# Token sums earlier in one lasting tile, portions ahead of PV, and a projection spread over five periods

## The chip, the cores and the metric

The kernel runs on one core of a Trainium2 chip. The core has a matrix engine (TensorE, PE in the profile, with PEld for its weight loads), VectorE (DVE), ScalarE (ACT), GpSimd (POOL) and SyncE (SP), each with its own queue[...]. DMAs are issued from the queues of SP and POOL. The metric is the device time of one execution in microseconds, the median of several runs.

## What is computed

Two cross-attention layers follow each other for 8 batch elements. Queries are 100 tokens of 640 channels in 20 heads of 32. The context has 722 tokens of 1024 channels: 77 are text, 645 are image tokens ("ip"). Keys and values of both kinds are projected with weights of their own, and there are two softmaxes per head, over text and over image tokens. Layer 1 adds a term to the image logits and multiplies the image probabilities with a mask. Cut to what matters:

```python
# layer 0, for H = 20 heads
q = split(x @ Wq.T);  k, v = split(text @ Wk.T), split(text @ Wv.T)
k_ip, v_ip = split(ip @ Wk_ip.T), split(ip @ Wv_ip.T)
x = (attend(q, k, v) + attend(q, k_ip, v_ip)) @ Wo.T + bo + x
# layer 1, the same with its own weights, and
q_sem = softmax(q_all @ k_text_all.T * scale) @ text
sem = (q_sem @ ip.T) * scale
ip_probs = softmax(q @ k_ip.T * scale + 0.5 * sem) * mask
out = (softmax(q @ k.T * scale) @ v + ip_probs @ v_ip) @ Wout + bout + x
```

All data are fp32.

## The kernel before

A unit u is one batch element in one layer: units 0 to 7 are layer 0, 8 to 15 layer 1. Units go in pairs (`PAIRS`, eight of them). There are two kinds of work, interleaved by hand on TensorE, VectorE and ScalarE.

**Production** makes keys and values of image tokens, for a pair at a time, and writes them to scratch in DRAM (`k_d`, `v_d`, by POOL's DMAs). Image tokens are cut into five blocks of 128 (the last 133). Each block's product is a 2x2 block product in Winograd's form with seven products instead of eight (`seven`, in the order first, sixth, second, seventh, fifth, fourth, third). The rows of the 2x2 are the two units of the pair, so the seven products need sums of the two units' tokens: S1 and S2 (`token_sums`, lines 232 and 233, on VectorE), S4 (`fourth_sum`), and S3, which overwrites a quarter of x (`third_sum`). S1 feeds the fifth product, S2 the sixth, S4 the third. Values are made per block (`v_steps`, line 605, tiles psv_a to psv_e), keys for blocks (0, 1), (2, 3) and (4) together (`k_steps`, line 633, tiles psk). Each product is followed by an eviction from PSUM (lines 193 to 224). The sums of a group of blocks stand in a tile `s` from a pool with one buffer, made anew for each group; x stands in three places of one tile, refilled by SP's DMAs (line 166). The last pair is made differently, in visits: `two_chunks` (line 775, tiles psvk, sums sl) ten times, and `fifth_chunk` (line 814, psv) five times.

**Attention** goes in 80 periods, one for four heads of a unit (`ORDER`). In a period n TensorE does: the scores' first part against 512 tokens (line 976), transposes 0 to 3 of the probabilities of the period before (line 1067), the scores' second part, transposes 4 and 5, then PV of the period before (`values`, line 1089). VectorE takes the maxima (line 991 in layer 1) and copies transposes (line 1074; 2 and 4 go to ScalarE, line 1072), ScalarE makes the exponentials (line 999, 1018). What turns exponentials into probabilities stands in a list `later`: "portions" that call `factors` (lines 1021 to 1025), `scaled_rest` (1035, 1039) on VectorE and `scaled` (1031) on ScalarE. A portion is emitted before each production task that takes time, and what is left is emitted at the next period's first scores.

Small work is put between, too: for each pair of units the output projection in five pieces (`out_piece`, line 887, tile pso) and in layer 0 the next query projection. For the second last pair, the five pieces stood in period 71. The last pair's projection (`last_out`, line 939) is in period 79 and at the end. A planner (`spread`) gives each production task a due time so that all periods of a stretch have about the same TensorE work, small work counted; `between` emits tasks up to a time. Periods 70 to 79 belong to the last pair; production for it ends about period 73 (two_chunks) and 79 (fifth_chunk).

Of the kernel before, what the change touches and what calls it, by code (L numbers as in the profile page):

```python
# [15 lines left out]
B = 8  # L16
# [28 lines left out]
def two_layer_xattn(  # L45
# [113 lines left out]

    def load_x(us, j):  # L160

        n0, n1 = BLOCKS[j]
        at = placed[0] % NPLACE
        placed[0] += 1
        for i, u in enumerate(us):
            nc.sync.dma_start(
                x_all[:, at, i, :, : n1 - n0], ip_t[u % B].rearrange("k p n -> p k n")[:, :, n0:n1]
            )
        return at

# [323 lines left out]
    def load_res(g):  # L494

        us = PAIRS[g]
        l, b = divmod(us[0], B)
        t = one.tile([P, 2, NC_, S], F32, tag="res", name=f"res_{g}")
        n = len(us)
        if l == 0:  # L500
            nc.sync.dma_start(t[:, :n], x_t[:, b : b + n])
        else:
            nc.sync.dma_start(t[:, :n], x1_d[b // 2][:, b % 2 : b % 2 + n])
        resg[g] = t
# [29 lines left out]

    places, pair_marks = {}, {}

    def pair_tasks(us):

        l = us[0] // B
        g = PAIRS.index(us)  # L540
        tasks, at = [], places.setdefault(us, {})
        marks = pair_marks[us] = {}

        def load(j, us=us):
            places.setdefault(us, {})[j] = load_x(us, j)

# [6 lines left out]
        for js in ((0, 1), (2, 3), (4,)):  # L553
            n = BLOCKS[js[0]][1] - BLOCKS[js[0]][0]
            st, pos = {}, {}

            def begin(j, js=js, n=n, st=st, pos=pos):
                if j == js[0]:
                    st[0] = spool.tile([P, 3, HK, 2, NX], F32, tag="s", name=f"s_{us[0]}_{j}")
                pos[j] = int(len(js) == 2 and (j == js[0]) == (at[js[0]] > at[js[1]]))  # L560
                sums = [st[0][:, i, :, pos[j], :n] for i in range(3)]
                a11, a12, a21, a22 = quarters(at[j], n)
                token_sums(a11, a12, a21, a22, sums[0], sums[1], None, sums[2])

            def fourth_sum(j, n=n, st=st, pos=pos):
                s2, s4 = (st[0][:, i, :, pos[j], :n] for i in (1, 2))
                nc.vector.tensor_tensor(s4, quarters(at[j], n)[1], s2, ALU.subtract)

            def operands(which, j, js=js, n=n, st=st, pos=pos):

                if which in (3, 5, 6):
                    t = st[0][:, {5: 0, 6: 1, 3: 2}[which]]
                    if j is not None:
                        return lambda k: t[:, k, pos[j], :n]
                    return lambda k: t[:, k, :, :n]
# [128 lines left out]
            if first:  # L704
# [6 lines left out]
                tasks += v[:2] + [(0.0, text_sum)] + v[2:] + v_steps(1)  # L711
            else:
                for j in js:
                    tasks += head(j) + with_sums(j, v_steps(j))
                    marks[f"v {j}"] = len(tasks)
                    if j == NB - 1 and us[0] + 2 < B:
                        tasks.append((0.0, lambda: load_text([u + 2 for u in us])))
                tasks += ([] if l else k4_steps()) + ks_
            marks[f"k {js[-1]}"] = len(tasks)

            then = {0: ((us, 3), (us, 4)), 2: ((PAIRS[g + 1], 0), (PAIRS[g + 1], 1)), 4: ((PAIRS[g + 1], 2),)}
# [17 lines left out]
    def last_visits(visits):  # L739

        xs, lists = {}, []
        for i, (j, tasks_of) in enumerate(visits):

            def begin(i=i):
                if i == 0:
                    xs.update(places[LAST])
                elif i + 2 < len(visits):
                    xs[i + 2] = load_x(LAST, visits[i + 2][0])

            first_sums, tasks = tasks_of(j, xs, i)  # L750
            if first_sums and i:

                t, f = lists[-1][-1]
                lists[-1][-1] = (t, lambda f=f, g=first_sums: (f(), g()))
            lists.append([(0.0, begin)] + ([(0.0, first_sums)] if first_sums and not i else []) + tasks)
        return lists

    def two_chunks(r, j, xs, at):
        n0, n1 = BLOCKS[j]
# [3 lines left out]
        def begin():  # L763
            t = spool.tile([P, 3, HK, 2, NX], F32, tag="s", name=f"sl_{r}_{j}")
            a11, a12, a21, a22 = quarters(xs[at], n)
            s1, s2, s4 = (t[:, i, :, 0, :n] for i in range(3))
            sums.update(token_sums(a11, a12, a21, a22, s1, s2, None, s4))
            sums[7] = a21
            late.append(lambda: nc.vector.tensor_tensor(a21, a11, a21, ALU.subtract))
            late.append(lambda: nc.vector.tensor_tensor(s4, a12, s2, ALU.subtract))  # L770
            o[0] = opool.tile([P, 2, 2, P + NX], F32, tag="made", name=f"vko_{r}_{j}")

# [12 lines left out]
        def step(i):  # L785
            if i == 0:
                made[0] = seven(
                    f"psvk_{r}_{j}", product, tuple(o[0][:, h, m, : P + n] for h in range(2) for m in range(2))
                )
# [15 lines left out]

    def fifth_chunk(j, xs, at):
        open_ = {}

        def half(h):
# [3 lines left out]
            for k in range(NCC):  # L813
                nc.tensor.matmul(
                    ps[:, h * P : (h + 1) * P], lhsT=x_all[:, xs[at], h, k, :P],
                    rhs=wide[("wv00", "wv10")[k // HK]][:, k % HK, 2 * P : 3 * P],
# [5 lines left out]
            nc.scalar.copy(t, ps[:, : 2 * P].rearrange("p (i n) -> p i n", i=2))  # L822
            for i, u in enumerate(LAST):
                nc.gpsimd.dma_start(v_d[u][j * P : (j + 1) * P, 4 * P :], t[:, i])

# [48 lines left out]

    def load_wo(kind, src, g):
        for c in range(NC_):
            t = wpool.tile([P, NC_, P], F32, tag="wo", name=f"{kind}_{g}_{c}", bufs=3)
# [85 lines left out]
    def scores(u, c, part):  # L963
        k0, k1 = ((0, KA), (KA, NK))[part]
        if part == 0:
            emit(len(later))
            pr[u, c] = ppool.tile([S, 4, NK], F32, tag="p", name=f"p_{u}_{c}")
# [108 lines left out]
    def values(u, c):  # L1076
        g, at = group_of[u]
        if g not in hsg:
            hsg[g] = one.tile([P, 2, NC_, S], F32, tag="hs", name=f"hs_{g}")
        pt = pts[u, c]  # L1080
# [17 lines left out]
    def production():  # L1098
# [15 lines left out]
        def insert(i, *what):  # L1114
# [7 lines left out]
        v, k = asked("v", HC), asked("k", 2 * P)  # L1122
        insert(
            B // 2 - 1,
            ("v 4", 0, [(0.0, lambda: load_wv(wvi[1]))]),
            ("k 4", 1, v[:1]),
            ("k 4", 0, v[1:2] + [(0.0, lambda: load_quarters("k", wki[1], 2 * P))]),
        )
        insert(
            B // 2,  # L1130
            ("v 0", 7, v[2:3]), ("v 0", 6, v[3:]),
            ("v 1", 7, k[:1]), ("v 1", 6, k[1:2]), ("v 1", 5, k[2:3]), ("v 1", 3, k[3:]),
        )

        v_last = asked("v", 2 * P)
        insert(len(PAIRS) - 2, ("v 4", 0, [(0.0, last_weights)]), ("k 4", 2, v_last[:1]), ("k 4", 1, v_last[1:2]))
        for i, tasks in enumerate(all_tasks):
            plan.append((10 * i - AHEAD, 10 * i + 10 - AHEAD, tasks))
        n = 5 * LAST[0]
        every = list(range(NB))  # L1140
        visits = [(j, lambda j, xs, i, r=r: two_chunks(r, j, xs, i)) for r in range(2) for j in every]
        visits += [(j, fifth_chunk) for j in every]
        lists = last_visits(visits)

        lists[0][5:5] = v_last[2:3]
        lists[0][7:7] = v_last[3:]
        for a, b, tasks in (
# [35 lines left out]
    def small_work(n):  # L1183
# [21 lines left out]
        if n == len(ORDER) - 1:  # L1205
            for i in range(2):
                for ks_ in ((0, 1), (2, 3)):
                    at[2 * i + ks_[0] // 2].append((2.3, lambda i=i, ks_=ks_: last_out(i, ks_)))

        if u % 2 == 0 and 0 < u <= LAST[0]:  # L1210
            g = u // 2 - 1
            if p == 1:
                for i, c in enumerate(range(NC_)):
# [6 lines left out]
    def loads(n):  # L1220
        u, p = divmod(n, NC_)
        if u % 2 == 0 and 0 < u <= LAST[0]:
            g = u // 2 - 1
            if p == 0:
                load_wo("o", wo[PAIRS[g][0] // B], g)
            if p == 1 and g < B // 2:
                load_wo("q", wq[1], g)
        if n == NC_ * LAST[0] + 2:
            load_res(len(PAIRS) - 1)
# [16 lines left out]
    with tc.manual_schedule(engines={mybir.EngineType.PE, mybir.EngineType.DVE, mybir.EngineType.Activation}):  # L1246
        for _, f in pair_tasks(PAIRS[0]):
            f()
        load_q(0)
        load_vt(0)  # L1250
        load_k(0, 0)
        todo = production()
        done = [0]
# [35 lines left out]
        for n, (u, c) in enumerate(ORDER):  # L1289
# [15 lines left out]
            if n == NC_ * LAST[0] - 1:  # L1305
                load_q(LAST[1])
            between(n, 0.6, 0.8, at[2])
            if n < len(ORDER) - 2:
# [3 lines left out]
            if last:  # L1312
                transposes(*last, 4)
                transposes(*last, 5)
            between(n, 0.8, 1.0, at[3])
            if last:
                values(*last)
# [54 lines left out]
```

## Time and profile before

| | us |
|---|---|
| median of 3 runs | 2088.62 |
| lowest, highest | 2087.55, 2089.88 |
| profiled execution, whole | 2089.18 |
| its span, first to last instruction | 2087.4 |
| TensorE busy in it | 2041.9 (98%) |
| VectorE busy | 1119.4 (54%) |
| ScalarE busy | 785.1 (38%) |
| mean granted TensorE clock | 0.994 |

The busy time of matmuls is modelled[...]; so the share is no measure of how much work there is. The granted clock is that which the throttle allowed. "A <- B" in a list of waits means that an instruction of A stood still until one of B was done. In the chain of waits each step is the one that released the next. Second-layer production begins about 1108 us, production for the last pair about 1750 us, and the first scores of periods 71, 74 and 79 stand at 1948.42, 1995.10 and 2056.54 us.

### The profile page before, as it was taken

How to read it: one execution, taken by the hardware profiler on the slowest of the kernel's cores; microseconds unless marked ns; L12 is line 12 of the kernel's file. 1: busy time of each engine (PE TensorE's matmuls, PEld its weight loads, DVE VectorE, ACT ScalarE, POOL GpSimd, SP SyncE). 2: the span in 40 equal slices, each digit the busy share in tenths (PEclk: the TensorE clock that was granted, in tenths of full speed). 3: DMA queues.
4: the chain of work that ended last, by engine and by line, in shares of the span. 5: the costliest groups of instructions: out<-in, count | busy, mean ns of one | idle time of the engine just before them, and what ended most of it. 6: DMA issues, size and time to landing. Idle time of an engine off the chain costs nothing.

```text
span 2087.4 us, 38776 instructions
## 1 busy us (share of the span) xinstructions
PE 2041.9 (98%) x15154; PEld 1578.1 (76%) x15154; DVE 1119.4 (54%) x3053; ACT 785.1 (38%) x2255; POOL 309.1 (15%) x445
## 2 busy tenths in 40 slices
PE   9999999999999999999999999999999999999988
PEld 8676767776777877777777877786777678888866
DVE  2211222355555555555557566656565657777775
ACT  1001000134433333334433444434444445565565
POOL 3212312121111111111110011000101011111110
PEclk9999999999999999999999999999999999999998
DMA  9545223332422624225263443344333455545451
GB/s 329 151 133 168 81 74 94 94 95 82 112 84 87 169 78 119 83 81 162 75 166 116 142 127 108 94 135 122 111 103 110 114 141 142 164 126 146 125 152 38
DMA packets 296341, 252.20 MB, mean 121 GB/s; under 512 B 46623, under 2 KB 265171, under 8 KB 296159
## 3 DMA queue, kind: packets, MB, share of 16 engines
q1 hardware_dynamic: 274382, 181.29, 32.1%
q0 software_dynamic: 21776, 68.44, 9.2%
q8 instruction: 119, 1.95, 0.4%
q14 instruction: 64, 0.52, 0.1%
HBM read 180.74 MB, written 68.93 MB: 120 GB/s over the span
## 4 chain that ended last, share of the span: by engine, by line
PE 92%; DVE 5%; ACT 1%; issue 1%; DMA 0%; SPq 0%; DVEq 0%; ACTq 0%
PE psv_d L605 8%; PE pspt L1067 8%; PE psv_a L605 7%; PE psk_a L633 6%; PE psk_d L633 6%; PE sc L976 6%; PE pv L1089 5%; PE psv_e L605 4%; PE psv_b L605 4%; PE psv_c L605 4%; PE psk_c L633 3%; PE psk_b L633 3%; PE psk_e L633 3%; PE pso L887 3%; PE psk_d L666 2%; PE psq L275 2%
## 5 line engine op out<-in xcount | busy, mean ns | idle before, releaser
L999 ACT ACTIVATE p<-sc,st 100x512 f32<-100x512 f32 (+1 forms) x320 | 165.5, 529 | 216.8 <-DVE st L985 134.6
L1031 ACT ACTIVATE p<-p,st 100x512 f32<-100x512 f32 x320 | 207.6, 713 | 66.0 <-DVE st L1025 65.8
L1067 PE MATMUL pspt<-ident,p 100*128 100x100 f32 (+1 forms) x1920 | 217.6, 254 | 13.9 <-ACT p L1031 5.5
L1067 PEld LDWEIGHTS pspt<-ident,p 100*128 100x128 f32 (+1 forms) x1920 | 191.4, 139 | 52.0 <-ACT p L1031 8.6
L1074 DVE COPY pt<-pspt 128x400 f32<-128x400 f32 (+1 forms) x319 | 174.9, 568 | 103.5 <-PE pspt L1067 96.1
L999 ACT ACTIVATE p<-p,st 100x512 f32<-100x512 f32 (+1 forms) x320 | 176.6, 554 | 87.2 <-DVE st L991 87.2
L1072 ACT COPY pt<-pspt 128x400 f32<-128x400 f32 x161 | 79.1, 491 | 284.4 <-PE pspt L1067 284.0
L605 PE MATMUL psv_a<-wv,x 128*128 128x397 f32 (+1 forms) x560 | 185.5, 473 | 0.0
L654 POOL DMA_DIRECT2D k_d<-ko x140 | 99.5, 715 | 509.9 <-DVE ko L219 455.4
L605 PE MATMUL psv_d<-wv,s 128*128 128x320 f32 (+1 forms) x560 | 174.3, 454 | 0.0
L605 PEld LDWEIGHTS psv_a<-wv,x 128*128 128x128 f32 x560 | 103.1, 190 | 67.6 <-issue 12.6
L991 DVE CUSTOM_DVE_ANT_0 p<-sc,sem 100x512 f32<-100x512 f32 (+1 forms) x320 | 138.7, 490 | 20.0 <-PE sc L976 18.9
L605 PEld LDWEIGHTS psv_d<-wv,s 128*128 128x128 f32 x560 | 104.2, 190 | 54.7 <-issue 4.3
L976 PE MATMUL sc<-k,q 32*100 32x210 f32 (+1 forms) x1280 | 140.0, 507 | 0.9 <-DMA k<-k_d 0.9
L985 DVE TENSOR_REDUCE st<-sc 100x2 f32<-100x1024 f32 (+1 forms) x160 | 125.2, 824 | 28.6 <-PE sc L976 28.6
L620 POOL DMA_DIRECT2D v_d<-vo x70 | 38.8, 554 | 661.9 <-DVE gst L595 328.9
L633 PE MATMUL psk_d<-s,wk 128*128 128x256 f32 (+1 forms) x672 | 136.5, 348 | 0.0
L633 PE MATMUL psk_a<-x,wk 128*128 128x256 f32 (+1 forms) x672 | 135.7, 347 | 0.6 <-ACT ko L193 0.6
L633 PEld LDWEIGHTS psk_a<-x,wk 128*128 128x128 f32 x672 | 109.0, 189 | 21.3 <-issue 5.0
L633 PEld LDWEIGHTS psk_d<-s,wk 128*128 128x128 f32 x672 | 108.2, 189 | 18.5 <-issue 5.1
L605 PE MATMUL psv_b<-wvt,s 128*128 128x320 f32 x280 | 83.0, 439 | 11.5 <-DVE s L233 11.4
L605 PE MATMUL psv_e<-wvt,x 128*128 128x397 f32 (+1 forms) x280 | 92.6, 473 | 0.0
(227 smaller groups left out, 3319.8 us busy)
## 6 DMA issues: line engine op xcount, KB each, us to landing
x<-ip_t SPq DMA_DIRECT2D x80, 512.0 KB
k<-k_d SPq DMA_DIRECT2D x80, 322.5 KB
v<-v_d SPq DMA_DIRECT2D x80, 320.0 KB
v_d<-vo POOLq DMA_DIRECT2D x70, 320.0 KB, 2.6
k_d<-ko POOLq DMA_DIRECT2D x112, 128.0 KB, 4.8
o<-wo SPq DMA_DIRECT2D x35, 320.0 KB
x<-ip_t SPq DMA_DIRECT2D x20, 532.0 KB
q<-wq SPq DMA_DIRECT2D x20, 320.0 KB
```

The costliest lines, as they stand in the source:

```text
L605: nc.tensor.matmul(ps[:, :m], lhsT=tokens(k)[:, :P], rhs=w[:, k, :], start=(k == 0 and not go_on), stop=(k == HK - 1), skip_group_check=True,)
L633: nc.tensor.matmul(ps[:, i * m : (i + 1) * m], lhsT=W["k", WHICH[which]][:, k, r * P : (r + 1) * P], rhs=tokens(k), start=(i == 0 and k == ...
L654: nc.gpsimd.dma_start(dst[:, :, r], ko[0][:, h, :, i, p0 : p0 + n])
L976: nc.tensor.matmul(scs[i // 2][:S, i % 2, : k1 - k0], lhsT=qs_[u][rows, c, :], rhs=ks[u, c][rows, k0:k1], start=True, stop=True)
L985: nc.vector.tensor_reduce(st[:, part, 2 * h : 2 * h + 2], scs[h][:S, :, :n], AX.X, ALU.max, negate=True)
L991: nc.vector.tensor_tensor_reduce(out=p[:, i, k0 : k0 + n], in0=scs[h][:S, i % 2, :n], in1=sems[u][:, k0 : k0 + n], scale=-1.0, scalar=3.0e ...
L999: nc.scalar.activation(dst, dst if l else scs[h][:S, i % 2, :n], AF.Exp, bias=st[:, part, i : i + 1], scale=-1.0 if l else 1.0, accum_out= ...
L1031: nc.scalar.activation(p[:, i, :KA], p[:, i, :KA], AF.Copy, scale=mul[:, 0, i : i + 1])
L1067: nc.tensor.transpose(ps[:rows, i * S : (i + 1) * S], pr[u, c][:, i, j * P : j * P + rows], ident[:S, :S])
L1072: nc.scalar.copy(dst, src)
L1074: nc.vector.tensor_copy(dst, src)
L1089: nc.tensor.matmul(ps[32 * i : 32 * i + 32, :S], lhsT=lhs, rhs=pt[:rows, j, i * S : (i + 1) * S], start=(j == 0), stop=(j == 5),)
```

## The change

Five edits, with 30 lines more in all.

- The sums' tile `s_all` is made once and lasts. `head(j)`, which makes S1 and S2 of a block, is put two products ahead: a group's first head before the last two products of the group before (for the first group of a pair, of the pair before), a second block's head before the last two products of the first block. The visits of the last pair do the same. Some sums of weights move by a product to make room.
- The list of portions is emptied just before `values`, and no longer at the next period's first scores.
- From period 74 on, transposes 4 and 5 come straight after the second scores, ahead of the production or small work that is due there.
- The five pieces of the second last pair's output projection go one each into periods 74 to 78, and its weights are loaded one each in periods 72 to 76. For this the last pair's PV results and residual get tiles that others no longer need (`qst` and `wk4`).
- `place_of` computes where a block of x lies instead of remembering it.

```diff
+    s_all = spool.tile([P, 3, HK, 2, NX], F32, tag="s", name="s")
...
-        t = one.tile([P, 2, NC_, S], F32, tag="res", name=f"res_{g}")
+        pool, tag = (one, "res") if g < len(PAIRS) - 1 else (wpool, "wk4")
+        t = pool.tile([P, 2, NC_, S], F32, tag=tag, name=f"res_{g}")
...
+    def place_of(us, i):
+        return (NB * PAIRS.index(us) + i) % NPLACE
...
-                if j == js[0]:
-                    st[0] = spool.tile([P, 3, HK, 2, NX], F32, tag="s", name=f"s_{us[0]}_{j}")
...
             else:
+                if js[0]:
+                    tasks[ahead:ahead] = head(js[0])
+                else:
+                    first_sums[us] = head(0)
                 for j in js:
-                    tasks += head(j) + with_sums(j, v_steps(j))
+                    v = with_sums(j, v_steps(j))
+                    if len(js) == 2 and j == js[0]:
+                        v[-2:-2] = head(js[1])
+                    tasks += v
...
             marks[f"k {js[-1]}"] = len(tasks)
+            ahead = len(tasks) - 2
...
-            if first_sums and i:
-                t, f = lists[-1][-1]
-                lists[-1][-1] = (t, lambda f=f, g=first_sums: (f(), g()))
+            elif sums:
+                lists[-1][-2:-2] = [(0.0, sums)]
...
-    def load_wo(kind, src, g):
-        for c in range(NC_):
+    def load_wo(kind, src, g, chunks=range(NC_)):
+        for c in chunks:
...
         if part == 0:
-            emit(len(later))
...
-            hsg[g] = one.tile([P, 2, NC_, S], F32, tag="hs", name=f"hs_{g}")
+            hsg[g] = one.tile([P, 2, NC_, S], F32, tag="hs" if g < len(PAIRS) - 1 else "qst", name=f"hs_{g}")
...
+        for i in range(1, len(PAIRS) - 1):
+            insert(i, *wants.get(i, []), ("k 4", 2, first_sums[PAIRS[i + 1]]))
...
+        if NC_ * LAST[0] + 4 <= n < NC_ * LAST[0] + 4 + NC_:
+            at[0].append((1.7, lambda: out_piece(len(PAIRS) - 2, n - NC_ * LAST[0] - 4)))
...
-            if p == 1:
+            if p == 1 and u < LAST[0]:
...
+        if NC_ * LAST[0] + 2 <= n < NC_ * LAST[0] + 2 + NC_:
+            load_wo("o", wo[1], len(PAIRS) - 2, [n - NC_ * LAST[0] - 2])
...
-            between(n, 0.6, 0.8, at[2])
+            few = n >= NC_ * LAST[0] + 4
+            if not few:
+                between(n, 0.6, 0.8, at[2])
...
                 transposes(*last, 4)
                 transposes(*last, 5)
+            if few:
+                between(n, 0.6, 0.8, at[2])
             between(n, 0.8, 1.0, at[3])
+            emit(len(later))
             if last:
                 values(*last)
```

## The prediction

> **What bounds the kernel now.** I read four views in this order: the page's busy shares, TensorE's waits, the stretches of the last periods, the chain of waits there. The page has TensorE busy 2041.9 us of a 2087.4 us span, and the chain is 92% TensorE. No matmul is added or removed by the change, so it can win only TensorE's idle time (45.5 us) and time lost to a reduced clock. The waits of TensorE say whose it is (total us, times, longest):
>
> ```profile
> PE psv_b L605 <- DVE s L233: 11.4, 8, 2.9
> PE pspt L1067 <- ACT p L1031: 5.5, 14, 1.3
> PE psq L275 <- DMA wq<-wq: 4.7, 1, 4.7
> PE pspt L1067 <- DVE pt L1074: 3.4, 5, 0.8
> ...
> PE psvk_b L775 <- DVE sl L233: 1.1, 1, 1.1
> ```
>
> The first and last rows are one thing: nine times the second product of a block stands still for the token sum S2 of VectorE, 12.5 us in all. The timeline shows the worst:
>
> ```profile
> 1108.06 2.34 PE L605 MATMUL psv_a<-wv,x 128*128 128x320 f32 x8
> 1113.27 2.39 PE L605 MATMUL psv_b<-wvt,s 128*128 128x320 f32 x8 [2.87 <-DVE s L233]
> ```
>
> The block before ended at 1107.2, its last eviction waited behind attention work until 1109.49, and S1 ran only at 1111.71.
>
> The transposes' rows lie in the last ten periods. The stretches there (length, busy PE, PEld, DVE, ACT, POOL with counts, then granted clock) show two losses, idle time and a clock below 1.00:
>
> ```profile
> 1982.80:1995.10 12.30, 10.76 (x141) 9.15 (x137) 9.04 (x35) 8.24 (x25) 3.99 (x6) 1.00 1.00 285
> 1995.10:2005.90 10.80, 9.38 (x120) 7.41 (x120) 8.44 (x31) 8.64 (x25) 0.92 (x2) 1.00 0.79 216
> 2005.90:2019.30 13.40, 11.36 (x125) 9.11 (x120) 9.21 (x34) 8.85 (x25) 1.21 (x3) 0.87 0.32 92
> 2019.30:2033.00 13.70, 10.92 (x108) 8.12 (x104) 9.24 (x34) 8.48 (x24) 0.00 (x0) 0.75 0.19 53
> ```
>
> The chain of waits through one such period (start, us, what) shows that TensorE isn't the bound there; VectorE is in every second step:
>
> ```profile
> 2004.12 0.58 DVE pt L1074
> 2004.75 1.28 PE pv L1089 x48
> 2006.06 0.26 DVE hs L1093
> 2006.32 0.38 DVE st L1021
> ...
> 2007.50 0.71 DVE p L1039
> 2008.22 0.39 DVE p L1035
> 2008.60 0.60 DVE p L991
> ...
> 2011.05 0.50 DVE pt L1074
> 2011.59 1.05 PE pspt L1067 x8
> 2012.63 0.54 PE sc L976 x8
> ```
>
> The portions (L1021 to L1035, 2.3 us) stand in VectorE's queue behind the copy of PV, though the text exponentials that they need ended at 2004.43 (ScalarE, 2003.98 + 0.45). So portions and the next maxima (4 x 0.61) run one after the other, after PV.
>
> [...] L1021 starts 1.8 us after its input is there, right behind hs. [...] here the sums' pool has one tile, and S1 (1111.71) comes after the last product of the old block (1107.2). [...] 0.75 granted in the emptiest period[...]. [...] S1 and S2 measure 0.68 and 0.69, and those are used.
>
> **The change part by part**, against the profiled run's 2087.4 us of span (2089.18 in all, 1.8 outside the span, 0.56 above the median of 2088.62).
>
> *Sums earlier, one lasting tile.* 43 of the 45 heads (35 + 10 on line 232; the first two stay) go two products ahead. The first S1 and S2 then need only product 5 and older ones, and their place on VectorE is right behind product 5's eviction, which waits for that product anyway: no new wait on TensorE's results. Two products are 4.4 us or more of TensorE work in a pair, 3.6 in the last visits, plus what attention lies between; the longest stall is 2.87. So all nine waits fit under it: -12.5; I keep 1 for leftovers, **-11.5**. What it puts in front: S1+S2 = 1.37 us ahead of the evictions of products 4 and 3, and in many blocks ahead of the portions. The cover is product 4 itself (2.2 us): product 5's eviction 0.45 and the sums 1.37 make 1.8. No row of TensorE waits on those evictions now. The data: x of the third or fourth block was asked for a whole block earlier, now five products (11 us) before use instead of seven; only the two first sums wait for x today (3.9 us, start). Nothing. Weight sums slip by one product: nothing, same cover.
>
> *Portions before PV.* In periods with production tasks they were out already; the order moves there in one place. In the last periods and the tail they leave the loop, while PV (1.28) and the next scores (1.05) run.
>
> *Projection over periods 74 to 78, transposes 4, 5 right behind the second scores.* Five pieces of 1.69 leave period 71 (1948.4 to 1970.3), with 1.9 us of stalls there (0.91 + 0.32 + 0.17 + 0.49). The planner levels: production slips by about one product, and one half of a fifth-chunk task (1.9) moves from 74 to 73. Until the scores of period 74: -8.45 - 1.9 - 0.66 (PV in 73) - 0.9 (the k wait) + 1.9 = **-10**. The k wait: in 73 the last product ended 1985.76, k landed 1995.1, 9.3 us. After, TensorE has 0.7+1.9+0.7+0.55+1.9+0.8+1.9+1.2 = 9.6 between, so about 0; without that cover up to +2.
>
> Then the loop, from the copy of transpose 5 (time 0): PV to 1.4, scores to 2.4; VectorE portions to 2.3, hs, maxima to 5.2; ScalarE's scaling 1.3 to 3.8. A period with the piece alone (74, 76): first transposes 4.1 to 4.8, fifth-chunk half to 6.7 over the two copies, second transposes to 7.4, then scores, 2.4 of maxima, copy: 3.5. Total 10.9. With half task and piece together in front (75, 77, 78): transposes at 6.0, their copies one after the other to 7.65, scores at 8.1: 11.6. From the scores of 74 to those of 79: 6.05 (74) + 11.5 + 10.9 + 11.5 + 11.5 + 4.9 = 56.3 against 61.4 (1995.10 to 2056.54): **-5**. The piece of 1.69 goes where VectorE gave 2.3 free; PV still waits about 2.4 for transpose 5's copy where no half task is left in front of it.
>
> *Tail.* Before, the scaling waited for hs until 2072.99, and the transposes trickled 2073.77 to 2075.6. Its input, the text exponentials, ended at 2070.2, and they had themselves waited for the copy of transpose 4 (2067.71), which stood behind a projection. After, both waits go, and the projection runs meanwhile. Scores of 79 to the transposes 15.8 instead of 17.2; 24 transposes 3.5 instead of 6.0 at full clock; the end 6.6 instead of 7.5: **-5**.
>
> *Clock.* The sums above are for full clock. Before, half clock cost about 7.8 in 2013 to 2058 (psv 3.6 and 3.4 for 2.05, transposes 1.6 for 0.85, scores, PV) and 2.6 in the tail. Bounds afterwards 0 and 12; stalls of 2.4 us remain in three periods, so I take about half: **+6**.
>
> *Queues.* The five out writes (100 KB) and weight loads (320 KB) move with the pieces; VectorE's addition (0.4) is in the loop above. The last pair's residual gets its own place and is loaded near 1393: SP then waits for x_d (issued 1393.15, 5.0 to landing), between issues at 1393.45 and 1398.26: nothing is late. The two bias additions (1.99) move with it to a POOL that is idle until 1413.7.
>
> Sum: -11.5 - 10 - 5 - 5 + 6 = -25.5. A second way, by idle time: from 1948.4 on 19.2 idle and 10.4 clock go, 15.7 idle and 6 clock stay (2.4 x 3 + 0.9 x 3 + ... and about 5 at the end), -7.9, with the sums -19.4. The two differ by what stuttering matmuls hide in busy time. I take -23.5 from the median: **2065 us**.
>
> **Rivals.** (A) The end keeps its length: VectorE (9.2 busy of some 11 in such a period) stays the bound, or the clock trips as often. For it: 10.9 to 11.6 is hardly under today's undisturbed 10.8 to 11.9. Against: five pieces then run inside. Left: the sums and a few us, -13: 2076. (B) The denser end keeps the full clock: -31, 2058. For: the trips follow periods with 2 to 2.8 us idle. Against: three stalls of 2.4. (C) Slower: the sums expose evictions. VectorE is 60 to 75% busy in the second layer; a chunk of maxima ahead of product 5's eviction pushes it, the sums and product 4's eviction together, and the next block's first product then waits up to 1.37. It decides from 23.5 / 1.37 = 17 exposed heads of 43; with 25 it is +11: 2100. Against: the same 1.37 stands today ahead of the second product's eviction. (D) The lasting tile tracks strided parts as one and the early sums wait for product 3 after all: then VectorE stalls in order and TensorE gains nothing there, -12: 2077. Against: the first sums read and write parts whose last readers are products 5 and 6.
>
> **Chances.** Forecast 0.56 (own range 2059 to 2071), A 0.17, B 0.14, C 0.05, D 0.05, no change worth measuring 0.03. Range **2057 to 2077**: it takes in A and B and leaves C out. A change of 0.2% (4 us) is about what can be told from none: faster 0.92, same 0.03, slower 0.05.
>
> **What will show it.** Right: rows of psv_b and psvk_b behind s gone from TensorE's waits; pspt behind p L1031 near nothing; the last five periods at 11 to 11.6 with a projection in each; span of the stretch before 1995 some 20 us shorter. Wrong: new rows of psv or psk behind vo or ko evictions (C), a wait for k in period 74 above 1 us, granted clock below 0.8 over the last 80 us (A).

## The result and the profile after

The changed kernel takes 2060.6 us (median of 4 runs, 2060.31 to 2061.25); the kernel before took 2089.25 beside it (4 runs, 2087.55 to 2090.11). The ratio is 0.9864, its 95% interval 0.9847 to 0.9881: 28.65 us less. The forecast said 2065.0.

The waits of TensorE after (total us, times, longest):

```profile
PE psq L279 <- DMA wq<-wq: 5.3, 1, 5.3
PE pspt L1080 <- DVE res L906: 3.8, 13, 1.1
PE psv_b L613 <- DVE wvt L135: 2.9, 1, 2.9
PE pv L1103 <- DVE pt L1087: 2.4, 3, 0.8
...
PE sc L989 <- DMA k<-k_d: 0.9, 1, 0.9
```

The rows of psv_b and psvk_b behind s are gone, and so is the row of the transposes behind ScalarE's scaling (5.5 us before, 14 times). No row of a product behind a vo or ko eviction is larger than 0.6 us. What is new is psv_b behind a sum of weights, 2.9 us in one piece. The row of the transposes behind res, the residual's addition, grew from 2.1 us to 3.8.

The page shows how much the span lost, and that TensorE's busy time lost 13.7 us (2041.9 before), although there are as many matmuls:

```profile
span 2058.5 us, 38749 instructions
PE 2028.2 (99%) x15154; PEld 1568.4 (76%) x15154; DVE 1118.0 (54%) x3053; ACT 785.0 (38%) x2255; POOL 310.2 (15%) x445
```

Busy time that falls without work falling speaks for matmuls at a higher clock, which the stretches show (before, the 40 matmuls pv<-pt,v of a period took 1.07 us at 1.00, from 2070.18, and 1.90 at 0.50, from 2054.38). These are periods 74 to 78 and the tail after (columns as before; the clock is the third last):

```profile
1976.08:1987.03 10.95, 9.17 (x114) 7.19 (x115) 7.42 (x28) 6.84 (x22) 1.80 (x3) 1.00 0.98 277
1987.03:1998.43 11.40, 11.05 (x135) 9.07 (x131) 10.10 (x38) 8.57 (x25) 0.87 (x2) 1.00 0.38 109
1998.43:2010.01 11.58, 9.39 (x119) 7.24 (x115) 9.10 (x34) 8.38 (x24) 1.64 (x3) 1.00 0.29 83
2010.01:2021.40 11.39, 11.04 (x134) 9.06 (x131) 10.08 (x38) 8.53 (x25) 1.79 (x3) 1.00 0.30 84
2021.40:2032.32 10.92, 9.52 (x119) 7.23 (x115) 9.20 (x34) 8.65 (x25) 1.79 (x3) 1.00 0.20 53
2032.32:2058.50 26.18, 21.03 (x264) 18.18 (x260) 14.66 (x48) 12.42 (x31) 0.00 (x0) 0.97 0.10 33
```

And the same two stretches before, each as a whole:

```profile
1995.10:2056.54 61.44, 51.67 (x568) 39.58 (x568) 45.26 (x167) 43.09 (x124) 4.27 (x8) 0.87 0.32 91
2056.54:2087.40 30.86, 24.91 (x264) 20.79 (x260) 14.86 (x48) 12.42 (x31) 0.00 (x0) 0.83 0.08 28
```

Every period of this loop (74 to 78) runs at 1.00, where 0.87 was granted before. The span's 28.9 us came from four places:

| us | before | after | difference |
|---|---|---|---|
| start to the first scores of period 0 | 407.9 | 407.2 | -0.7 |
| from there to the scores of period 74 | 1587.2 | 1568.9 | -18.3 |
| scores of 74 to scores of 79 | 61.44 | 56.24 | -5.2 |
| scores of 79 to the end | 30.88 | 26.23 | -4.7 |

### The profile page after: what moved, and what is told of

Same layout as the page of the kernel before. It is cut to its first block, busy times and chain, and to the rows that moved or that the text cites. A ratio compares the mean times of both kernels' runs of the same rounds, so it can differ in the third digit from the quotient of the medians.

```text
span 2058.5 us, 38749 instructions
## 1 busy us (share of the span) xinstructions
PE 2028.2 (99%) x15154; PEld 1568.4 (76%) x15154; DVE 1118.0 (54%) x3053; ACT 785.0 (38%) x2255; POOL 310.2 (15%) x445
## 5 line engine op out<-in xcount | busy, mean ns | idle before, releaser
L1080 PE MATMUL pspt<-ident,p 100*128 100x100 f32 (+1 forms) x1920 | 211.9, 250 | 8.2 <-DVE res L906 3.8
L1103 PEld LDWEIGHTS pv<-pt,v 128*32 128x32 f32 x3200 | 67.5, 110 | 26.8 <-issue 13.6
```

The lines of the kernel that those rows point to most:

```text
L1080: nc.tensor.transpose(ps[:rows, i * S : (i + 1) * S], pr[u, c][:, i, j * P : j * P + rows], ident[:S, :S])
L1103: nc.tensor.matmul(ps[32 * i : 32 * i + 32, :S], lhsT=lhs, rhs=pt[:rows, j, i * S : (i + 1) * S], start=(j == 0), stop=(j == 5),)
```

## The experiments

Each starts from the changed kernel, and none leaves out any part of the output. The medians are of 4 executions, of 20 for sums twice. They were taken in other sessions than the changed kernel's; the median of the kernel before, taken beside each, lay between 2088.53 and 2089.32 us. Differences of a us or two between the rows are therefore not clear.

| edit | us, median (lowest to highest) | ratio to before, 95% interval | to 74 | 74 to 79 | tail |
|---|---|---|---|---|---|
| sums alone | 2078.68 (2076.67 to 2082.82) | 0.9946 (0.9928 to 0.9964) | 1577.0 | 60.19 | 32.85 |
| sums and portions | 2061.87 (2060.66 to 2067.30) | 0.9877 (0.9858 to 0.9896) | 1577.4 | 53.24 | 27.53 |
| portions undone | 2067.47 (2065.89 to 2068.38) | 0.9889 (0.9874 to 0.9904) | 1568.9 | 57.66 | 30.37 |
| spreading undone | 2065.03 (2061.97 to 2066.76) | 0.9877 (0.9861 to 0.9892) | 1576.2 | 51.71 | 26.70 |
| transposes 4, 5 back | 2062.02 (2061.06 to 2063.10) | 0.9863 (0.9847 to 0.9880) | 1568.7 | 57.21 | 27.37 |
| heads late | 2069.47 (2067.55 to 2070.01) | 0.9906 (0.9892 to 0.9921) | 1578.3 | 56.24 | 26.06 |
| pool tile | 2161.59 (2159.70 to 2165.62) | 1.0354 (1.0339 to 1.0370) | 1663.2 | 56.23 | 26.19 |
| sums twice | 2085.90 (2083.52 to 2087.68) | 0.9985 (0.9978 to 0.9992) | 1593.4 | 56.25 | 26.52 |
| weight sums early | 2056.83 (2055.49 to 2056.91) | 0.9849 (0.9834 to 0.9863) | 1564.3 | 56.24 | 26.19 |
| piece late | 2061.76 (2060.72 to 2062.20) | 0.9873 (0.9858 to 0.9888) | 1568.9 | 56.01 | 26.18 |
| 2 maxima twice | 2065.65 (2064.57 to 2068.76) | 0.9888 (0.9871 to 0.9905) | 1568.9 | 64.08 | 26.54 |
| 4 maxima twice | 2079.91 (2076.98 to 2080.66) | 0.9955 (0.9940 to 0.9971) | 1566.6 | 73.23 | 27.91 |

The last three columns are from one profiled execution each: from the first scores to those of period 74, from there to those of 79, and on to the end.

**Sums alone.** The lasting tile and the early sums stay; portions, transposes 4 and 5 and the pieces go back.

```diff
         if part == 0:
+            emit(len(later))
...
-        if NC_ * LAST[0] + 4 <= n < NC_ * LAST[0] + 4 + NC_:
-            at[0].append((1.7, lambda: out_piece(len(PAIRS) - 2, n - NC_ * LAST[0] - 4)))
...
-            if p == 1 and u < LAST[0]:
+            if p == 1:
...
-            few = n >= NC_ * LAST[0] + 4
+            few = False
...
-            emit(len(later))
             if last:
                 values(*last)
```

> The changed kernel with three of its edits undone: portions are emitted at the next first scores again, the five pieces of the projection stand in period 71, transposes 4 and 5 stand where they stood. What is left is the lasting tile and the early sums. Theory: psv_b and psvk_b no longer wait for s, and nothing else moves, so about 9 to 10 us faster than before (2079 to 2080), with the granted clock in the last 80 us at about 0.85 as before. Rival 1, the early sums cost as much in late evictions as they save: 2087 to 2090. Rival 2, the tile and the sums bring the whole gain: 2061.

Measured 2078.68. The gain up to period 74 is 10.2 us (1587.2 to 1577.0). At the end of the kernel nothing got better: 60.19 and 32.85 us, with clocks of 0.91 and 0.76. The sums bring about 10 us, all before period 74.

```profile
1985.31:2045.50 60.19, 49.63 (x569) 37.79 (x569) 45.33 (x169) 42.87 (x124) 4.27 (x8) 0.91 0.34 93
2045.50:2078.35 32.85, 26.49 (x264) 21.97 (x260) 14.95 (x48) 12.42 (x31) 0.00 (x0) 0.76 0.08 27
```

**Portions undone.** Only the place of the portions goes back.

```diff
         if part == 0:
+            emit(len(later))
...
-            emit(len(later))
             if last:
                 values(*last)
```

> The changed kernel with one edit undone: the portions are emitted at the next first scores, behind PV. Theory: the 2.3 us of portions come back into the loop of each of the last five periods and into the tail, so the stretch from the first scores of period 74 to those of 79 grows from 56.2 to 64 to 68 us, the tail by 3, and half-clock windows return: 2072 to 2078. Rival, the packing of the projection alone made the end shorter and the place of the portions matters little: 2061 to 2064.

Measured 2067.47, between the two. The loop grew by 1.4 us only (57.66), the tail by 4.1 (30.37 at clock 0.94, of which the clock took up to 30.37 x 0.06 = 1.8). The reading that fits is that with a projection in each period the time that late portions leave idle is mostly filled, and that the tail has no such filling.

**Spreading undone.** The five pieces and their weight loads go back to period 71.

```diff
-            at[0].append((1.7, lambda: out_piece(len(PAIRS) - 2, n - NC_ * LAST[0] - 4)))
...
-            if p == 1 and u < LAST[0]:
+            if p == 1:
...
```

> The changed kernel with the five pieces of the projection back in period 71. Theory: 8.5 us of matmuls and about 2 us of stalls come back before period 74, the last five periods get shorter by only 4 to 6 us, since VectorE's loop is their bound and not TensorE, and the idle time there lets the clock fall again (3 to 6 us): 2066 to 2071. Rival 1, the periods are bound by TensorE and get shorter by all 8.5 us: 2061 to 2063. Rival 2, the clock is the main thing and falls as in the kernel before: 2072 or more.

Measured 2065.03, a little under the theory's range. Until period 74 it takes 7.3 us more, as the pieces are back there. The loop is 4.5 us shorter. Its periods, of which one shows a lower clock:

```profile
1983.94:1993.51 9.57, 9.13 (x121) 7.38 (x122) 7.83 (x31) 7.90 (x24) 0.17 (x1) 1.00 0.79 217
1993.51:2003.79 10.28, 9.33 (x125) 7.40 (x121) 9.11 (x35) 8.52 (x25) 1.06 (x3) 1.00 0.49 135
2003.79:2016.39 12.60, 10.64 (x108) 7.94 (x105) 10.12 (x38) 8.67 (x25) 0.90 (x2) 0.73 0.24 66
2016.39:2025.95 9.56, 9.12 (x125) 7.38 (x121) 8.25 (x32) 8.11 (x25) 1.07 (x2) 1.00 0.34 89
```

The undisturbed periods last 9.6 to 10.3 us instead of 10.9 to 11.4. The period at 0.73 lost up to 12.60 x 0.27 = 3.4 us to the clock. So at full clock the loop without pieces would take some 48.3, and the pieces lengthen it by about 8, nearly all of their own 8.45, although the changed kernel has a half task of production fewer in these periods (603 matmuls, 569 here; the pieces have 50, a half task 16). With the portions early, the loop hides nothing of the pieces. What the spreading saves is 4.4 us by the medians, and the period at 0.73 alone accounts for up to 3.4 of that.

**Transposes 4 and 5 back** behind the due production (`few = False`).

> The changed kernel with transposes 4 and 5 of the last six periods behind the half task again. Theory: ScalarE's second exponentials wait for the copy of transpose 4 again, which delays the portions by up to 2 us where a half task or projection stands there (periods 75, 77, 79): 2063 to 2067. Rival, the loop runs over VectorE's maxima and not over that copy: 2060 to 2062.

Measured 2062.02, at the edge of the rival's range. Loop and tail are a us longer each in the trace, but the ratio to before is that of the changed kernel (0.9863 and 0.9864): that this edit brings anything by itself is not shown.

**Sums and portions.** The early sums and the portions ahead of `values` stay; the pieces and their weight loads go back to period 71, and transposes 4 and 5 behind the due production (`few = False`).

> The changed kernel with the early sums and the portions ahead of PV, but the five pieces back in period 71 and transposes 4 and 5 behind the due production again. Theory: in a loop that isn't filled with pieces the portions' place is worth more than the 6.9 us that their undoing alone cost: 2066 to 2069, so 10 to 12 us less than with the sums alone (2078.7). Rival: without transposes 4 and 5 directly behind the second scores the portions bring little, since the copy of transpose 5 is late: 2072 to 2077.

Measured 2061.87, better than both expectations, and 1.3 us from the whole change. Three of its four runs lie at 2060.66 to 2062.77; the fourth, the profiled one at 2067.3, has a period at 0.73:

```profile
1995.07:2005.39 10.32, 9.22 (x124) 7.37 (x120) 9.13 (x35) 8.64 (x25) 1.07 (x3) 1.00 0.38 109
2005.39:2018.08 12.69, 10.84 (x109) 8.23 (x105) 8.81 (x33) 8.47 (x24) 0.13 (x1) 0.73 0.23 66
```

Up to period 74 it stands where the sums alone stand (1577.4 and 1577.0); all that the portions bring lies behind. On top of the sums, the portions' place is worth 16.8 us by the medians, and spreading and transposes after it 1.3, which is within the spread of the runs. In the other order spreading and transposes are worth 11.2 (2078.68 to 2067.47) and the portions 6.9. So the edits are no sum. Much of what either brings is clock: with the sums alone, loop and tail lost up to 13.3 us to it (60.19 x 0.09 + 32.85 x 0.24), and in the profiled sums and portions 4.3, which is up to 9 of the 12.3 us by which they got shorter.

**Heads late.** The lasting tile stays, S1 and S2 of each block go back to their old place; the visits' stay early.

```diff
-                if js[0]:
-                    tasks[ahead:ahead] = head(js[0])
-                else:
-                    first_sums[us] = head(0)
+                first_sums[us] = []
                 for j in js:
-                    v = with_sums(j, v_steps(j))
-                    if len(js) == 2 and j == js[0]:
-                        v[-2:-2] = head(js[1])
-                    tasks += v
+                    tasks += head(j) + with_sums(j, v_steps(j))
```

> The changed kernel with its lasting tile, but each block's S1 and S2 stand again where they stood before the change, directly ahead of the block's own products; the visits' sums stay early. Theory: the early place is what removes the waits, and the lasting tile only allows it: TensorE's waits of psv_b on s come back, 7 to 9 of them with 8 to 10 us in all, and the time is 2068 to 2071. Rival: the lasting tile alone frees the sums from the last product of the old group, and VectorE then makes them in time: at most 3 us of psv_b waits, 2060 to 2063.

Measured 2069.47, as the theory said. The old row stands there again, with the very numbers of before:

```profile
PE psv_b L613 <- DVE s L237: 11.4, 8, 2.9
```

**Pool tile.** The heads stay early, but each group, and each visit of the last pair, takes its tile from the pool with one buffer again.

```diff
-    s_all = spool.tile([P, 3, HK, 2, NX], F32, tag="s", name="s")
...
+                if j == js[0]:
+                    st[0] = spool.tile([P, 3, HK, 2, NX], F32, tag="s", name=f"s_{us[0]}_{j}")
...
```

> The changed kernel with the sums' tile taken from the pool for each group again (one buffer), heads still two products early. Theory: the first S1 of a group must wait for the last reader of the old tile, product 3, and VectorE's queue stands still behind it, so product 4's and product 3's evictions come late: product 3 can't finish... at best TensorE loses 1 to 3 us at each of some 20 group changes, 2080 to 2110. Rival, the pool's wait costs nothing since the queue has time: 2060 to 2064.

Measured 2161.59: the direction of the theory, but 101 us over the changed kernel where it had 19 to 49. The waits of VectorE (first row) and of TensorE show how:

```profile
DVE s L235 <- PE psk_d L643: 72.7, 19, 5.3
PE psv_a L615 <- DVE ko L222: 25.8, 12, 3.8
PE pv L1106 <- DVE pt L1090: 7.1, 5, 3.3
PE pspt L1083 <- ACT tp L857: 6.0, 6, 1.5
```

A sum that needs the whole tile free waits on VectorE for the last product of the old group. Behind it in VectorE's queue stand the evictions of the products before (ko) and the copies of attention (pt), and TensorE waits for those. That is the theory's mechanism; what it left out is the clock. The profiled run's mean granted clock is 0.985, against 0.999 in the changed kernel, so up to 32 us of its 2163.9 are lost to it, where the changed kernel loses 2. So the early place alone would have made the kernel slower; early place and lasting tile are one edit. In the kernel before, no row shows VectorE waiting for the tile: with the sums late, the one buffer cost nothing.

**Sums twice.** S1 and S2 of each head are made two times over: 45 x 1.37 = 61.7 us more of VectorE, in the early place.

```diff
+        if s3 is None:
+            nc.vector.tensor_tensor(s1, a21, a22, ALU.add)
+            nc.vector.tensor_tensor(s2, s1, a11, ALU.subtract)
```

> The changed kernel with S1 and S2 of each head made twice, 1.37 us more of VectorE in front of the evictions at 45 heads. Theory: product 4 and the slack of VectorE hide it but for the last pair's visits, where VectorE is 75 to 80% busy: plus 1 to 5 us, 2062 to 2066. Rival, the sums in front of the evictions are at the edge of being exposed: plus 20 us or more, 2080.

Measured 2085.9: the theory fell. Of each us of added VectorE work 0.41 came through (25.3 of 61.7), all of it before period 74, and the rows that the third rival named appear:

```profile
PE psv_a L616 <- DVE ko L223: 8.2, 7, 1.6
PE pv L1106 <- DVE pt L1090: 6.1, 7, 1.3
```

VectorE is 54% busy over the whole kernel, and yet 1.37 us at this one place fit and 2.74 don't.

**Weight sums early.** The first two of layer 1's value weight sums are made three products sooner, so that line 135 is done before psv_b needs it.

```diff
-                ("k 4", 1, v[:1]),
-                ("k 4", 0, v[1:2] + [(0.0, lambda: load_quarters("k", wki[1], 2 * P))]),
+                ("k 4", 4, v[:1]),
+                ("k 4", 3, v[1:2]),
+                ("k 4", 0, [(0.0, lambda: load_quarters("k", wki[1], 2 * P))]),
```

> The changed kernel with the first two sums of layer 1's value weights made three products earlier in the pair before (before product 5 and 4 of its last keys instead of before and after the last one). Theory: the one wait left in front of psv_b (2.9 us, for the weight sum of line 135 and not for the token sum) goes, and with it the half-clock window that follows: 2 to 4 us faster, 2057 to 2058.6. Rival, the weights' load hasn't landed by then and VectorE stands for it: 2062 or more.

Measured 2056.83, the fastest of all kernels here: 3.8 us under the changed one, and its slowest run 3.4 us under the fastest of that. By the ratios it is 3.1, with intervals that overlap; the trace is the firmer ground. Up to period 74 it gains 4.6 (1568.9 to 1564.3): the wait of 2.9, and up to 3.41 x 0.5 = 1.7 for the 3.41 us at half clock that came behind it in the changed kernel (last section; here 1.00 is granted from 1100 to 1120). The changed kernel there (start, us, then what; TensorE, and VectorE ahead of it):

```profile
1106.11 1.48 DVE L134 TENSOR_TENSOR wvt<-wv,wv 128x1280 f32<-128x1280 f32 x1
1109.41 0.43 DVE L228 TENSOR_TENSOR ko<-psk_d,ko 128x266 f32<-128x266 f32 x1
1110.24 1.48 DVE L135 TENSOR_TENSOR wvt<-wvt,wv 128x1280 f32<-128x1280 f32 x1
```

```profile
1106.65 2.34 PE L613 MATMUL psv_a<-wv,x 128*128 128x320 f32 x8
1111.86 3.82 PE L613 MATMUL psv_b<-wvt,s 128*128 128x320 f32 x8 [2.86 <-DVE wvt L135]
```

S1 and S2 had ended at 1105.9 already. The eight matmuls after the stall took 3.82 us; in the run with the early weight sums the same eight take 2.31, with no stall:

```profile
1110.09 2.31 PE L613 MATMUL psv_b<-wvt,s 128*128 128x320 f32 x8
```

**Piece late.** The projection of a period goes behind the second scores (`at[3]`) instead of to its start (`at[0]`).

> The changed kernel with each of the five pieces of the projection in periods 74 to 78 behind transposes 4 and 5 instead of in front of transposes 0. Theory: it fills TensorE's wait for the copy of transpose 5 (about 1.7 us idle between the transposes and the text part of PV in periods 74, 76, 78), and takes VectorE's addition out of the way of the copies (2.6 us of waits for res there): 3 to 6 us faster, 2055 to 2058. Rival, its two PSUM buffers are those of the transposes and PV, so PV waits for the addition and the portions start later: 2060 to 2063.

Measured 2061.76: the rival's range. The row of the transposes behind res fell from 3.8 us to 1.4, and other rows grew for it (behind the copies pt from 0.5 to 3.3); the loop stayed at 56.01. Taking away the instruction that a row names did not take away the wait. That the pieces' PSUM buffers are the reason, as the rival has it, is not shown.

**Maxima twice.** Two, then four of the four maxima of the first scores are made again in periods 74 to 79.

```diff
         for h in range(2):
             maxima(h)
+            if part == 0 and ORDER.index((u, c)) >= NC_ * LAST[0] + 4 and h < 1:
+                maxima(h)
```

> The changed kernel with two of the four 512-element maxima of the first scores made twice in periods 74 to 79, 1.22 us more of VectorE in each. Theory: VectorE still bounds the filled loop, each period grows by about 1.2 and the tail too: periods 74 to 79 62.3 instead of 56.2, time 2066 to 2069 with a half-clock window or two. Rival: the projection now fills the loop and TensorE bounds it, with slack of a us or more on VectorE: periods 74 to 79 at most 58.5, time 2061 to 2064.

> As the run before, with all four maxima twice: 2.44 us more of VectorE in each of periods 74 to 79. Theory: periods 74 to 79 at 68.4, tail 2.4 longer, and, as the stalls of TensorE grow to some 4 us, half-clock windows return: 2075 to 2082. Rival: the first us or so is slack: periods 74 to 79 at 62 to 65, 2067 to 2073, full clock.

Measured 2065.65 and 2079.91: the times that the theory named, the first a little under its range, but not by its sum. The loop took 64.08 and 73.23, with these clocks:

```profile
1976.38:2040.46 64.08, 53.35 (x602) 42.80 (x602) 51.88 (x188) 41.97 (x122) 7.89 (x13) 0.95 0.38 107
```

```profile
1974.07:2047.30 73.23, 57.85 (x607) 46.96 (x603) 58.20 (x208) 43.03 (x123) 7.91 (x13) 0.88 0.33 92
```

Taking off what the clock cost at most (64.08 x 0.05 = 3.2 and 73.23 x 0.12 = 8.8) leaves 60.9 and 64.4, that is 4.7 and 8.2 more than 56.24 for 6.1 and 12.2 us of VectorE work in five periods: some 0.7 us for each us, where the theory had 1. The clock made up the rest; at full clock the second loop would lie in the rival's 62 to 65. VectorE still bounds most of the loop, but not all of it. A stall of the second kernel shows where it comes out:

```profile
2010.94 0.56 PE L1082 MATMUL pspt<-ident,p 100*128 100x100 f32 x4 [3.17 <-DVE res L906]
```

## Why the prediction was right, and where it was off

**Sums: -11.5 forecast; measured 9.6 by the waits that went, 10.2 by the stretch up to period 74.** Eight of the nine waits went, and heads late brings those back (8.9 us). The step that failed is "the first and last rows are one thing: nine times the second product of a block stands still for the token sum S2". The ninth and longest, at 1113.27 before, was listed behind S2. But psv_b also needs the weight sum of line 135, which ended 1.3 us before S2, and both stood in one stretch in which the view shows no pause of VectorE:

```profile
1103.19 0.57 DVE L1074 COPY pt<-pspt 128x400 f32<-128x400 f32 x1 [0.26 <-PE pspt L1067]
...
1110.32 1.48 DVE L135 TENSOR_TENSOR wvt<-wvt,wv 128x1280 f32<-128x1280 f32 x1
1112.43 0.69 DVE L233 TENSOR_TENSOR s<-s,x 128x512 f32<-128x512 f32 x1
```

After, the stretch begins with the same copy and ends with line 135, which runs from 1110.24 to 1111.72, again without a pause in the view:

```profile
1101.79 0.57 DVE L1087 COPY pt<-pspt 128x400 f32<-128x400 f32 x1 [0.25 <-PE pspt L1080]
```

psv_b starts 10.08 us after that copy before, and 10.07 us after it in the changed kernel. S1 and S2 moved to the front of a stretch without gaps and pushed line 135 back by as much as they take, so the wait kept its 2.9 us and got another name. The forecast's term for the weight sums ("nothing, same cover") looked at those that slip by a product and not at this one. Taking lines 134 and 135 out of that stretch, to where VectorE still had pauses of over 1 us, is what makes the fastest kernel.

**What stands ahead of the evictions: nothing forecast, nothing measured.** No new row. But the forecast's reasoning about cover (1.8 us under product 4's 2.2) leaves 0.4 us, and sums twice agrees that it is thin. The third rival named the right mechanism; its price only isn't paid at 1.37 us. Of the fourth, a tile tracked as one, nothing is seen: VectorE's sums wait for no product in the changed kernel.

**Until the scores of 74: -10 forecast; 18.3 less the sums' 10.2 leaves 8.1.** Two terms are off. The wait for k was to go and stayed at 0.9: the cover was as counted, from the end of the last product at 1965.7 to 1975.2, 9.5 us, but k came only at 1976.08, after 10.4 us instead of 9.3. The rest, about 1 us, is smaller than what one trace resolves.

**The loop: 56.3 forecast, 56.24 measured.** The sum is closer than its parts. Periods 74 and 76 were forecast at 10.9 and lasted 10.95 and 11.58; 75, 77 and 78 were forecast at about 11.6 and lasted 11.40, 11.39 and 10.92. So 76 took 0.7 more and 78 took 0.7 less, and the two cancel: that is luck. (78 had as many matmuls as 76, 119, and not as many as 75 and 77.) The order of the steps in period 76 is the one worked out: portions, hs, maxima, then the copies, then the second transposes.

```profile
1997.75 0.47 DVE st L1034
...
1999.03 0.71 DVE p L1052
1999.74 0.39 DVE p L1048
2000.13 0.17 DVE hs L1107
2000.30 0.60 DVE p L1004
...
2002.74 0.35 DVE res L906
2003.09 0.04 issue
2003.13 0.56 PE pspt L1080 x4
2003.70 1.81 PE psv L828 x16
2005.51 0.70 PE pspt L1080 x8
```

What the forecast's sentence on the pieces got wrong is who hides whom: "the piece of 1.69 goes where VectorE gave 2.3 free". Moving the portions forward uses these 2.3 us up: with portions early and no pieces, undisturbed periods last 9.6 to 10.3. Worked through in one period both were counted together, so the 56.3 came out right although that sentence was not.

**Tail: -5 forecast, -4.7 measured.** From the scores of 79 to the last transposes 15.9 (2032.32 to 2048.24; forecast 15.8), and 24 transposes in 3.3 (forecast 3.5). Sums alone has none of this gain, sums and portions most of it (27.53).

**Clock: +6 forecast, at most 0.8 measured** (26.18 x 0.03; the loop is at 1.00). This is the mis-sized term, and more than the forecast's whole error of 4.4 us; the second rival, with its full clock and 2058, was nearer. The forecast took stalls of 2.4 us in three periods as enough to lower the clock. What came in periods 74, 76 and 78 was 1.8, 2.2 and 1.4 us of idle time, in single stalls of at most 1.1, and the clock did not fall. In before, sums alone, spreading undone and the profiled sums and portions, the clock falls in the loop (0.87, 0.91, 0.93 and 0.94 granted); in the changed kernel, portions undone, transposes back, piece late and weight sums early, which have pieces in it and no added work, it doesn't (1.00). Against that, the clock fell once where no term of the forecast had it, at the ninth wait, at 1111.34 us (0.50 granted for 3.41 us).

In the profiled execution of before, the falls lie whole multiples of 3.413 us apart (at 2013.34, 2023.58, 2050.89, 2074.78 and 2085.02), and so do the two of the changed kernel (last section). In the 3.41 us ahead of the five, TensorE was idle for 1.01, 2.22, 1.37, 1.39 and 1.78 us. Divided at the same step, counted back from its fall at 2056.84, the changed kernel's loop has at most 1.05 us of idle time in one stretch (2029.53 to 2032.94); the 2.2 us of period 76 are shared out among several, with at most 0.92 in one (2002.22 to 2005.64). For the loop that fits the full clock; but 1.01 us went ahead of a fall before and 1.05 of none after, so that the exact reason there stays open. Four maxima twice, with single stalls of up to 3.2 us, was granted 0.89 in each of periods 74 to 77 and 0.86 in 78.

**The sum.** The terms without clock came to -31.5; measured are -28.9, with the clock's 0.8 in them, so -29.7 without. The terms promised 1.8 too much, the clock took 5 too much away, and leaning toward the second way of counting another 2: the errors partly cancelled. One reading of the prediction is off without effect: line 1021 starts 1.9 us after its input is there (2004.43 to 2006.32), not 1.8.

## What to carry to other kernels

When a wait of the critical engine is to be removed, list every operand of the waiting instruction and when each one was ready, since the row names only the last. Then look whether the queue that makes them has a gap ahead of them: in a stretch without gaps, an operand that is moved forward pushes back the others. Two edits that fill the same idle time are not added; work them through together, and undo each alone, and both, before saying what either brought. To make something earlier in a queue, first make sure that it needn't wait there: late sums gave 2069.47 us, and the same sums made early gave 2060.60 in a lasting tile and 2161.59 in a pool with one buffer.

## What the runs showed of the hardware

- In the profiled executions of before and of the changed kernel, TensorE's clock was lowered five times and twice, always to 0.50. Before, that lasted 3.41 us from 2013.34, 6.83 each from 2023.58, 2050.89 and 2074.78, and from 2085.02 past the end; after, 3.41 us from 1111.34, and from 2056.84 past the end. The two falls after lie 945.49 us apart, 277 times 3.413.
- Two stalls of the same length differed in what came with them. Before the change TensorE stood still for 2.87 us up to 1113.27, and the clock stayed at 1.00; in the changed kernel it stood still for 2.86 us up to 1111.86, and the clock was at 0.50 from 1111.34 to 1114.76. Divided at steps of 3.413 us counted from the falls, 1.82 and 1.05 us of the first stall lie in two stretches (with the border at 1112.22), and 2.34 us of the second lie in one. The third last column is the granted clock, first before, then after:

```profile
1108.81:1112.22 3.41, 1.59 (x6) 0.76 (x5) 3.38 (x6) 2.99 (x5) 1.41 (x2) 1.00 0.86 273
```

```profile
1107.93:1111.34 3.41, 1.07 (x4) 0.40 (x3) 3.27 (x9) 2.56 (x5) 0.97 (x2) 1.00 0.65 216
1111.34:1114.76 3.42, 2.90 (x6) 1.95 (x7) 1.37 (x3) 0.32 (x1) 0.45 (x1) 0.50 0.46 114
```

- The eight matmuls behind the stall took 2.39 us before and 3.82 after (2.31 in weight sums early, without a stall). The stretch up to period 74 took 1568.9 us in the changed kernel and 1566.6 in four maxima twice, though nothing was changed in it; why is not shown.
- In these two executions, from 50 us on and at full clock, some of these stretches of 3.41 us were followed by half clock. Of those without transposes in them, the ones with 2.34 us of idle time (after, from 1107.93), 2.23 (after, from 2053.42) and 1.78 (before, from 2081.61) were, by the modelled busy time, and one with 1.82 (before, from 1108.81) was not. Of those with transposes, the ones with 1.01, 1.37, 1.39 and 2.22 (before, from 2009.93, 2047.48, 2071.37 and 2020.17) were, and those with 1.24 (before, from 1951.90) and 1.05 (after, from 2029.53) were not. The amount of idle time alone does not separate the two here.
- The same program lost unequal time to the clock from one execution to the next: of four of sums and portions, one took 2067.3 us at a mean granted clock of 0.996, the others 2060.7 to 2062.8 at 0.999 to 1.000.
